# Graph attention on one core: another order for the products of the last pairs

## The chip, the cores and the metric

The kernel runs on one core of a Trainium2 chip. The metric is the device time of one execution in microseconds; the time before is the median of six runs. A core has TensorE (PE in the profile, its weight loads PEld), VectorE (DVE), ScalarE (ACT), GpSimd (POOL) and SyncE (SP), which here issues most DMAs and loads the registers that these DMAs take their addresses from.

## The reference

One layer of graph attention over 12,500 nodes with 256 features in 8 heads of 32, and 200,000 edges sorted by destination. The part that matters:

```python
h = maximum(layernorm(x), 0)
q, k, v = h @ Wq + bq, h @ Wk + bk, h @ Wv + bv        # 8 heads of 32
logits = sum(q[dst] * k[src], axis=-1) / sqrt(32)
expv = exp(logits - segment_max(logits, dst)[dst])
agg = segment_sum(expv / segment_sum(expv, dst)[dst] * v[src], dst)
out = agg + (h @ Wskip + bskip)
y = h + gelu(out)
result = x + layernorm(y) * gamma + beta
```

The last three lines, done for 128 nodes at a time, are what the change reorders at the end of the kernel.

## The kernel before, in words

First `project` makes h and the rows of k and v and stores them in the tables `h_tab` and `kv_tab`, while `make_plan` turns the edge list into indices. Then `walk_streams` goes over the edges. The edges are cut into 8 streams of 25,000, and each stream into chunks of 383 new edges, 66 chunks in all (`NST`, c from 0 to 65). A chunk is three tiles of 128 edges; the last one (c = 65) has only two (`KL`).

For each chunk GpSimd gathers rows of k and v (L1006), VectorE multiplies them with queries that TensorE has spread over the edges (L1039, L1049), sums them to logits (L1058), and takes running maxima of them (L1078 to L1081). TensorE transposes the logits before that (L1067) and the exponentials after it (L1089). VectorE multiplies v with the weights (L1105, L1110), and TensorE adds the weighted rows up per node (`add_up`, L1124), in three groups i = 0, 1, 2. ScalarE copies each group's sums to `sums_w` (L1133) and the last row on to the next chunk (L1139), and SyncE stores them to `table` in HBM (L1143). The addresses of these stores come from `nodes(c)`, a load of registers.

When the sums of 256 nodes are known to be complete, a `Pair` of two blocks of 128 nodes finishes them: sums, x and h are fetched (L797 to L799), and then

- `turn`: four transposes of h to PSUM (L812) and a copy to `hT` on ScalarE (L815)
- `divisors`, `divide`: VectorE divides the sums by the weights' sums (L804, L806, L818)
- `skip`: TensorE puts the bias (L825) and the product of hT with Wskip (eight matmuls, L829) into a PSUM bank
- `add`, `gelu`: four matmuls with the identity add the divided sums to that bank (L834), and ScalarE takes gelu (L838)
- `stats`, `root`, `factors`, `normal`: mean and variance on VectorE (L841 to L847), square root on ScalarE (L851), L855 and L856 on VectorE, the normalised rows on ScalarE (L861)
- `shifted`, `scale`, `store`: x + beta in PSUM (L868, L871), L875 and L877 on VectorE, and two stores to `out` by SyncE (L882)

There are 52 pairs, numbered 0 to 51. From chunk 10 on, a pair's fetch is put into a chunk, most of its work into the following one, and its end (`factors` to `store`) into the one after that. Pairs 0 to 45 are done in this way. In the loop's last iteration (c = 64) `before` is pair 43, `pair` is pair 44 and `pair_next` is pair 45. In the code after the loop, for chunk 65, `before` is pair 44 and `pair` is pair 45. Six pairs are left (46 to 51, called leftover 0 to 5 here), of the class `Last`, in the list `lasts`. Their sums are complete only when chunk 65 is stored. Their x and h are fetched during chunk 64 (`fetch_rows`, into buffers of the gathers that are no longer used), their sums after chunk 65's stores (`fetch_sums`, L909).

The order of all instructions but the gathers is written out by hand. `keep` ties every instruction to the one before it on the same engine, so each engine works strictly in the order of the code, and an instruction that waits holds up all that stands behind it on its engine. SyncE too takes its register loads (`loaded`, L770), its waits and its DMAs in the order of the code.

[...] A tile from `hot_ps` waits until the tile two allocations earlier has been read. The leftovers' products go to `qe_ps` (leftovers 0 to 3), `xt_ps` (4) and `ag_ps` (5); pair 45's product goes to `ag_ps`. Transposes of h, `shifted` and parts of `add_up` use `hot_ps`. The buffer `hT` of a pair has one copy (`bufs=1`), so a copy to it waits for the matmuls of the product before.

ScalarE has to load another table of functions when it goes from one function to another (1.28 us each, ACT_TABLE_LOAD in the timeline); `table_of` asks for such a load ahead of its use by a one-element instruction.

Of the kernel before, what the change touches and what calls it, by code (L numbers as in the profile page):

```python
# [38 lines left out]
P = 128  # L39
# [5 lines left out]
S = 8  # L45
# [695 lines left out]
def walk_streams(tc, N, HID, NST, KL, ident, idx, d0_row, slot_row, near, near_n, e_tab, pen_tab, h_tab,  # L741
# [32 lines left out]
    class Pair:  # L774


        own, depth = "", 2
# [30 lines left out]
        def turn(self):  # L808
            ps = self.ps_h()
            for b in range(2):  # L810
                for c in range(KC):
                    self.keep(nc.tensor.transpose(ps[:, b, c, :], self.h[:, b, c * P:(c + 1) * P],  # L812
                                                  ident))
            self.hT = self.pool.tile([P, 2, KC, P], F32, name="hT", bufs=1)
            self.keep(nc.scalar.copy(self.hT, ps))  # L815
# [63 lines left out]
        def store(self, b):  # L879
            if b == 0:  # L880
                self.nodes = loaded(slot_row[0:1, self.m, 0:2], N - P)
            self.keep(nc.sync.dma_start(out[ds(self.nodes[b], P), :], self.y[:, b, :]))  # L882

    class Last(Pair):

        own, depth = "_l", 4
# [14 lines left out]
        def fetch_rows(self):  # L901
            self.places()
            for b, node in enumerate(loaded(slot_row[0:1, self.m, 0:2], N - P)):
                self.keep(nc.sync.dma_start(self.x[:, b, :], x[ds(node, P), :]))
                self.keep(nc.sync.dma_start(self.h[:, b, :], h_tab[ds(node, P), :]))

        def fetch_sums(self):
            for b, row in enumerate(loaded(slot_row[0:1, self.m, 2:4], S * NT - P)):
                self.keep(nc.sync.dma_start(self.sums[:, b, :], tab[ds(row, P), :]))  # L909

    rest = []
    with ExitStack() as es:
# [199 lines left out]
        def add_up(c, i, tiles=range(K)):  # L1112
# [3 lines left out]
            if tiles[0] == 0:  # L1116
                g["ps", i] = (hot_ps.tile([P, 2 * HID], F32, name="ps_hot")
                              if i == 1 or i == 2 and c == NST - 1 else
                              ag_ps.tile([P, 2 * HID], F32, name="ps_a"))[:, :SUMS]
# [87 lines left out]
        for c in range(NST - 1):  # L1207
# [78 lines left out]
            add_up(c, 1)  # L1286
            if pair:
# [34 lines left out]
        if pair:  # L1322
            pair.turn()
            pair.divisors()
            pair.skip()
# [10 lines left out]
        for p in lasts[:2]:  # L1336
            p.turn()
            p.skip()
# [4 lines left out]
        weigh(c, tiles_of(c) - 1)  # L1343
        for i in range(3):
# [3 lines left out]
        for p in lasts:  # L1348
            p.fetch_sums()
        if pair:  # L1350
# [7 lines left out]
        for p in lasts[2:]:  # L1358
# [5 lines left out]
        for p in lasts:  # L1364
# [3 lines left out]
            p.gelu()  # L1368
        table_of(AF.Sqrt)
# [356 lines left out]
```

## Time and profile before

| | us |
|---|---|
| median of the six runs | 2408.04 |
| lowest and highest of them | 2404.53, 2420.95 |
| the profiled execution, its own time | 2412.02 |
| its span | 2410.2 |

Busy time by engine, from the page:

| engine | busy us | share of the span |
|---|---|---|
| TensorE matmul | 1885.8 | 78% |
| VectorE | 1934.9 | 80% |
| GpSimd | 1592.0 | 66% |
| ScalarE | 1078.6 | 45% |

TensorE's granted clock has two levels in this trace, 1.00 and 0.50; its mean over the span is 0.874. Eight matmuls of L829 took 1.99 us in a stretch at 1.00 and 3.78 us in one at 0.50.

The marks of the end, from the timeline, in us from the span's start:

| start | what |
|---|---|
| 2320.54 | L1124, group 1 of chunk 64 (1.56) |
| 2326.34 | L1124, group 2 of chunk 64 (2.91) |
| 2333.47 | L812, transposes of pair 45 |
| 2336.54 | L1082, chunk 65's exponentials (0.42) |
| 2339.67 | L1105, chunk 65's first tile |
| 2346.97 | L1124 of chunk 65, until 2350.29 |
| 2349.75 | L1143, first store of chunk 65's sums |
| 2359.22 | L909, first fetch of the leftovers' sums |
| 2370.14 | L834, add of leftover 0 |
| 2377.43 | L838, gelu of leftover 5 (0.60) |
| 2383.39 | L882, first store of the leftovers |
| 2405.41 | L882, last store |

In the timeline a line gives start, duration, engine, line, operation and tiles. SPq is SyncE's queue; PEld is a weight load, which overlaps the matmuls. The idle time before an instruction stands in brackets with what ended it.

### The profile page before, as it was taken

What the parts mean: (1) busy time and instruction counts of PE and PEld (TensorE: products, weight loads), DVE (VectorE), ACT (ScalarE), POOL (GpSimd) and SP (SyncE); (2) the same over time, 40 slices, a digit from 0 to 9 for tenths busy, and PEclk for the clock granted to TensorE, in tenths of its full rate; (3) what the DMA queues carried; (4) which work ended last, traced back from release to release, by engine and by line L of the source; (5) the groups of instructions that cost most, each with busy time, mean ns of one, the idle gap of its engine ahead of it and who ended that gap; (6) DMA issues with size and microseconds to landing.
All of it is one profiled execution on the core that took longest, in us unless ns stands there. A gap on an engine that the chain in (4) does not pass through costs nothing.

```text
span 2410.2 us, 34981 instructions
## 1 busy us (share of the span) xinstructions
PE 1885.8 (78%) x10240; PEld 1090.5 (45%) x10240; DVE 1934.9 (80%) x2228; ACT 1078.6 (45%) x2527; POOL 1592.0 (66%) x1646
## 2 busy tenths in 40 slices
PE   7999677778877777787787777877787778887775
PEld 3444444344544444444454444544444444444443
DVE  7888577778788888788778888788777888888864
ACT  3432233333455455454445454454454554544433
POOL 2210677777777777777777777777777777777720
PEclk9999768777899899899989898899888998889877
DMA  7865777778787887888878888788878888888852
GB/s 275 302 250 205 235 244 243 244 244 253 251 276 245 266 262 245 265 270 258 265 240 260 260 266 260 244 274 261 265 246 264 257 263 258 264 254 262 254 159 68
DMA packets 274030, 601.06 MB, mean 249 GB/s; under 512 B 47239, under 2 KB 164212, under 8 KB 271648
## 3 DMA queue, kind: packets, MB, share of 16 engines
q0 software_dynamic: 128736, 423.23, 56.2%
q1 hardware_dynamic: 144562, 175.02, 21.8%
q8 instruction: 84, 1.38, 0.2%
q14 instruction: 118, 0.97, 0.1%
q10 hardware_dynamic: 530, 0.47, 0.1%
HBM read 514.42 MB, written 84.11 MB: 248 GB/s over the span
## 4 chain that ended last, share of the span: by engine, by line
POOL 29%; DMA 21%; DVE 15%; issue 15%; PE 15%; ACT 4%; SPq 0%; DVEq 0%; ACTq 0%; POOLq 0%
POOL kv L1006 28%; DMA kv<-kv_tab,idx 17%; DVE vw L1105 5%; PE ps_kv L243 5%; DVE prod L1049 4%; PE ps_qe L1039 3%; DVE L L1058 2%; DMA table<-sums_w 1%; PE ps_a L829 1%; DMA x_in<-in_x_dram 1%; DVE st L845 1%; PE ps_hot L871 1%; PE ps_hot L999 1%; PE ps_a L1124 1%; DMA e_tab<-row 1%
## 5 line engine op out<-in xcount | busy, mean ns | idle before, releaser
L1006 POOL DMA_INDIRECT kv<-kv_tab,idx x1576 | 1548.7, 983 | 524.6 <-issue 431.6
L1039 PE MATMUL ps_qe<-qw,to_e 64*128 64x256 f32 x3152 | 475.4, 431 | 220.6 <-DVE prod L1049 220.5
L1105 DVE TENSOR_TENSOR vw<-ps_x,kv 128x2048 f32<-128x2048 f32 x197 | 444.6, 2284 | 173.7 <-ACT vw L1098 172.1
L1049 DVE TENSOR_TENSOR prod<-ps_qe,kv 128x1024 f32<-128x1024 f32 x394 | 467.5, 1219 | 120.5 <-DMA kv<-kv_tab,idx 104.3
L1039 PEld LDWEIGHTS ps_qe<-qw,to_e 64*128 64x128 f32 x3152 | 302.5, 203 | 374.8 <-DVE prod L1049 334.7
L1058 DVE TENSOR_REDUCE L<-prod 128x64 f32<-128x2048 f32 x197 | 450.4, 2286 | 6.7
L999 PE MATMUL ps_hot<-w_q,hwT 128*128 128x256 f32 x792 | 256.7, 470 | 1.0 <-ACT hwT L985 0.8
L1124 PE MATMUL ps_a<-vw,to_n 128*32 128x264 f32 (+1 forms) x2356 | 219.6, 399 | 2.7 <-DVE vw L1105 1.5
L999 PEld LDWEIGHTS ps_hot<-w_q,hwT 128*128 128x128 f32 x792 | 169.7, 230 | 90.7 <-issue 60.7
L243 PE MATMUL ps_kv<-w_kv,hT 128*128 128x512 f32 x392 | 186.8, 620 | 21.8 <-ACT hT L136 20.8
L1029 ACT ACTIVATE to_n<-ps_hot,ones 128x384 f32<-128x384 f32 x197 | 107.2, 579 | 212.7 <-PE ps_hot L1027 210.5
L1133 ACT COPY sums_w<-ps_a 128x264 f32<-128x264 f32 x131 | 49.7, 379 | 325.8 <-PE ps_a L1124 325.8
L946 ACT ACT_TABLE_LOAD x138 | 177.1, 1283 | 2.4
L1001 ACT COPY qw<-ps_hot 128x256 f32<-128x256 f32 (+1 forms) x132 | 63.3, 480 | 253.5 <-PE ps_hot L999 251.5
L1139 ACT COPY kv<-ps_a 1x264 f32<-1x264 f32 x390 | 144.1, 369 | 6.4
L1018 ACT ACTIVATE to_e<-ps_hot,ones 128x384 f32<-128x384 f32 x264 | 143.7, 587 | 6.8 <-PE ps_hot L1016 6.6
L1124 PEld LDWEIGHTS ps_a<-vw,to_n 128*32 128x32 f32 (+1 forms) x2356 | 88.5, 118 | 123.9 <-issue 75.7
L985 ACT COPY hwT<-ps_hot 128x256 f32<-128x256 f32 (+1 forms) x132 | 63.5, 481 | 166.7 <-PE ps_hot L982 162.8
L829 PE MATMUL ps_a<-w_s,hT 128*128 128x256 f32 x376 | 123.1, 483 | 12.9 <-ACT hT L815 10.4
L1016 PE MATMUL ps_hot<-et,near 48*128 48x384 bf16 x264 | 90.2, 342 | 42.2 <-ACT qw L1001 25.7
L243 PEld LDWEIGHTS ps_kv<-w_kv,hT 128*128 128x128 f32 x392 | 72.0, 194 | 105.8 <-issue 72.1
L1089 PE MATMUL ps_x<-ident,W 64*128 64x64 f32 x197 | 31.0, 275 | 98.1 <-ACT W L1082 98.1
(289 smaller groups left out, 2189.2 us busy)
## 6 DMA issues: line engine op xcount, KB each, us to landing
kv<-kv_tab,idx POOLq DMA_INDIRECT x1576
kv_tab<-kvo SPq DMA_DIRECT2D x14, 1536.0 KB
table<-sums_w SPq DMA_DIRECT2D x264, 65.0 KB
hw<-h_tab SPq DMA_DIRECT2D x264, 64.0 KB
pen<-pen_tab SPq DMA_DIRECT2D x66, 192.5 KB
sums<-table SPq DMA_DIRECT2D x92, 132.0 KB
x_f<-in_x_dram SPq DMA_DIRECT2D x92, 128.0 KB
h<-h_tab SPq DMA_DIRECT2D x92, 128.0 KB
```

What stands on the lines that cost most here:

```text
L243: ins = nc.tensor.matmul(ps_kv, hT[:, c, :], w_kv[:, c, :], start=c == 0, stop=c == KC - 1)
L829: self.keep(nc.tensor.matmul(self.ps[:, b, :], self.hT[:, b, c, :], w_s[:, c, :], start=False, stop=False, skip_group_check=True))
L946: keep(nc.scalar.activation(dummy[:, 1:2], dummy[:, 0:1], function))
L999: keep(nc.tensor.matmul(ps[:, b, :], g["hwT"][:, b, k, :], w_q[:, k, :], start=False, stop=k == KC - 1, skip_group_check=True))
L1006: nc.gpsimd.indirect_dma_start(out=t[:, s, :], out_offset=None, in_=kv_tab[:, :], in_offset=bass.IndirectOffsetOnAxis(ap=idx[:, s, j, c:c ...
L1018: keep(nc.scalar.activation(step[c]["to_e"][:, i, :], ps[:, :CH], AF.Relu, scale=-1.0, bias=ones))
L1039: keep(nc.tensor.matmul(ps[:, b, a, :], g["to_e"][r, 2 * half + a, j * P:(j + 1) * P], g["qw"][r, (half + a) * half, :], start=True, stop= ...
L1049: keep(nc.vector.tensor_tensor(g["prod"][:, four, :].rearrange("p (a b) d -> p a b d", a=2), g["qe", half].rearrange("p b a d -> p a b d") ...
L1058: keep(nc.vector.tensor_reduce(g["L"][:, j, :].rearrange("p (s h) -> p s h", s=S), g["prod"].rearrange("p s (h d) -> p s h d", h=HEADS), A ...
L1105: keep(nc.vector.tensor_tensor(t[:, :, HEADS:].rearrange("p s (h d) -> p s h d", h=HEADS), wj[:, :, :, None].to_broadcast([P, S, HEADS, D] ...
L1124: keep(nc.tensor.matmul(ps[at:at + w, :], g["to_n"][:, j, i * P + at:i * P + at + w], g["vw"][j][:, s, :], start=j == 0, stop=j == tiles_o ...
L1139: keep(nc.scalar.copy(step[c + 1]["kv"][0][0:1, s, HID - HEADS:], ps[at:at + 1, :]))
```

## The change

It concerns the end alone: chunk 64's second half and all that follows. No arithmetic is added or removed.

- Pair 45's transposes and its product with Wskip (`turn`, `skip`) move from the code after the loop into the loop's last iteration, behind group 1 of `add_up` for chunk 64. Group 2 of chunk 64 takes a tile of `hot_ps` and not of `ag_ps`.
- Leftover 0's transposes move ahead of chunk 65's maxima, its product stays behind pair 45's gelu; leftover 1's transposes follow that, and its product moves behind chunk 65's `add_up`, together with transposes and products of leftovers 2 and 3. Leftover 4 stays where leftovers 2 to 5 were, behind pair 45's end. Leftover 5's come after the gelu of leftover 1.
- The leftovers have four buffers for hT, of their own.
- The registers with the places of the leftovers' sums are loaded ahead of chunk 65's last `add_up` (`find_sums`), and the registers with the node numbers, loaded for the fetch of x and h, are kept for the stores.

```diff
     class Pair:
-        own, depth = "", 2
+        own, depth, turned = "", 2, 1
...
-            self.hT = self.pool.tile([P, 2, KC, P], F32, name="hT", bufs=1)
+            self.hT = self.pool.tile([P, 2, KC, P], F32, name="hT" + self.own, bufs=self.turned)
...
         def store(self, b):
-            if b == 0:
+            if b == 0 and not self.own:
                 self.nodes = loaded(slot_row[0:1, self.m, 0:2], N - P)
...
     class Last(Pair):
-        own, depth = "_l", 4
+        own, depth, turned = "_l", 4, 4
...
         def fetch_rows(self):
             self.places()
-            for b, node in enumerate(loaded(slot_row[0:1, self.m, 0:2], N - P)):
+            self.nodes = loaded(slot_row[0:1, self.m, 0:2], N - P)
+            for b, node in enumerate(self.nodes):
...
+        def find_sums(self):
+            self.rows = loaded(slot_row[0:1, self.m, 2:4], S * NT - P)
+
         def fetch_sums(self):
-            for b, row in enumerate(loaded(slot_row[0:1, self.m, 2:4], S * NT - P)):
+            for b, row in enumerate(self.rows):
...
-                              if i == 1 or i == 2 and c == NST - 1 else
+                              if i == 1 or i == 2 and c > NST - 3 else
...
             add_up(c, 1)
+            if c == NST - 2 and pair_next:
+                pair_next.turn()
+                pair_next.skip()
             if pair:
                 pair.stats()
...
         if pair:
-            pair.turn()
             pair.divisors()
-            pair.skip()
+        for p in lasts[:1]:
+            p.turn()
         maxima(c)
...
             pair.add()
             pair.gelu()
-        for p in lasts[:2]:
+        for p in lasts[:1]:
+            p.skip()
+        for p in lasts[1:2]:
             p.turn()
-            p.skip()
...
         weigh(c, tiles_of(c) - 1)
+        for p in lasts:
+            p.find_sums()
         for i in range(3):
             add_up(c, i, range(tiles_of(c) - 1, tiles_of(c)))
         if before:
             before.store(1)
         for p in lasts:
             p.fetch_sums()
+        for p in lasts[1:2]:
+            p.skip()
+        for p in lasts[2:4]:
+            p.turn()
+            p.skip()
...
             table_of(AF.Gelu)
-        for p in lasts[2:]:
+        for p in lasts[4:5]:
             p.turn()
             p.skip()
...
-        for p in lasts:
+        for i, p in enumerate(lasts):
             p.divisors()
             p.divide()
             p.add()
             p.gelu()
+            if i == 1:
+                for p in lasts[5:]:
+                    p.turn()
+                    p.skip()
```

## The prediction

> **What bounds the kernel now.** I read the page's chain of waits first, to see whether the change touches what sets the time of the loop.
>
> ```profile
> POOL kv L1006 28%; DMA kv<-kv_tab,idx 17%; DVE vw L1105 5%; PE ps_kv L243 5%; DVE prod L1049 4%; PE ps_qe L1039 3%; DVE L L1058 2%; DMA table<-sums_w 1%; PE ps_a L829 1%; DMA x_in<-in_x_dram 1%; DVE st L845 1%; PE ps_hot L871 1%; PE ps_hot L999 1%; PE ps_a L1124 1%; DMA e_tab<-row 1%
> ```
>
> The loop runs at the pace of the gathers (L1006 and their landing, 45% of the span). The change leaves them alone, and by the timeline the last gather is over by 2308. So only the end counts, from about 2320 to 2410.2, some 90 us of 2410.
>
> Second, SyncE's queue and its own waits from 2370 on (waited for: us in total, times, longest).
>
> ```profile
> 2383.39 22.35 SPq L882 DMA_DIRECT2D out_dram<-kv  x12
> SPq L882 <- DMA out_dram<-kv: 13.4, 11, 2.3
> SPq L882 <- DVE kv L877: 11.2, 1, 11.2
> ```
>
> The page's chain of waits stops at 2396.46, with the last L877, and so hides what really ends the span. The twelve stores of the leftover pairs go out one at a time: eleven waits, each for the store before to land. The first goes out at 2383.39, when the first leftover pair's L877 ends; the last at 2405.41; the span ends 4.8 us later. So the end is the first leftover store + 22.0 + 4.8, and the question is how much earlier the first L877 comes.
>
> Third, the chain of waits between 2350 and 2378 (start, us, what).
>
> ```profile
> 2353.89 1.28 ACT L946
> 2355.18 0.20 ACT dummy L946
> 2355.38 0.47 ACT hT L815
> 2355.90 2.79 PE ps_qe L829 x8
> ...
> 2359.63 0.59 ACT hT L815
> 2360.27 3.71 PE ps_qe L829 x8
> ...
> 2365.15 1.99 PE ps_x L829 x8
> ...
> 2368.31 1.99 PE ps_a L829 x8
> 2370.30 0.88 PE ps_qe L834 x4
> ...
> 2377.43 0.60 ACT kv L838
> ```
>
> What leads to that first store is TensorE with ScalarE: transposes, copy of hT, eight matmuls with Wskip, pair after pair. The sums are no part of it: the first L818 (divide) ends at 2363.21, while its add (L834) waits in TensorE's order until 2370.14.
>
> Fourth, TensorE's busy time and granted clock in stretches between clock changes (us; busy and count of PE, PEld, DVE, ACT, POOL; clock; DMA share; GB/s).
>
> ```profile
> 2322.82:2326.23 3.41, 0.11 (x1) 0.11 (x1) 3.34 (x4) 2.28 (x5) 0.00 (x0) 1.00 0.61 184
> 2326.23:2329.65 3.42, 3.42 (x15) 1.35 (x14) 0.01 (x1) 0.33 (x2) 0.00 (x0) 0.50 0.40 132
> 2329.65:2333.06 3.41, 1.29 (x6) 0.77 (x5) 0.69 (x1) 2.73 (x7) 0.00 (x0) 1.00 0.32 90
> 2333.06:2336.47 3.41, 3.27 (x10) 2.06 (x9) 2.65 (x7) 0.59 (x1) 0.00 (x0) 0.50 0.18 60
> 2356.95:2360.37 3.42, 3.23 (x11) 1.91 (x9) 0.00 (x0) 0.59 (x1) 0.00 (x0) 0.50 0.06 16
> 2360.37:2363.78 3.41, 3.41 (x8) 2.65 (x9) 1.29 (x4) 0.00 (x0) 0.00 (x0) 0.50 0.63 169
> ```
>
> After a stretch with little work the next runs at 0.50, and twelve L1124 matmuls take 2.91 us there against 1.56 just before. The hole at 2322 is where the change puts work.
>
> **The change, step by step.** All times are on the clock of this execution. It took 2412.0 us (span 2410.2, 1.8 outside); the median of the runs is 2408.04, 4.0 lower. I take the gain off both.
>
> (1) Pair 45's transposes and product move into the hole. TensorE is free at 2322.10; transposes 0.60, bias matmul 0.39 (full-clock rows). The copy of hT (0.59) queues on ScalarE behind L1139, which ends at 2323.45: done by 2324.05, product (1.99) until 2326.05; L1067 needs the engine at 2326.12. It costs nothing with 0.07 to spare; at half clock (3.78) it delays L1067 by 1.8. On ScalarE root and the table load slide by 0.6, under the idle 4.16 before L1133 at 2329.32. The PSUM bank of ag_ps is then held until pair 45's gelu, which is why L1124's last group for chunk 64 takes a bank of hot_ps; the two tiles before it there are already copied. The hole filled, those twelve matmuls should run at full clock: 2.91 becomes 1.56, **1.35 gained** (bounds: 1.35 gained, 1.8 lost). I take the gain, as 2.35 of 3.41 us is then busy, nearer to the stretches that keep the clock.
>
> (2) With that product gone from 2334 to 2339, the transposes back (L1089) no longer wait. Exp ended at 2336.96 and the first L1105 began at 2339.67. Now what follows Exp is ScalarE's own queue: table load 1.28, dummy 0.20, L1096 0.23, L1098 0.21, so L1105 starts 1.9 after Exp instead of 2.7: **0.8 gained**, 2.15 together. It starts at 2337.5.
>
> (3) TensorE then does pair 45's add (1.79 at half clock, row at 2307.80), leftover 0's product, leftover 1's transposes, and then L1124; leftover 1's product moves behind. Add from 2336.1 to 2337.9; product partly at half clock until 2341.1; transposes until 2341.8. L1124 starts there and not at 2346.97: 5.2 earlier, **3.05 more**. VectorE's weights are ready (second L1105 over by 2342.1; the second half of L1124 starts at 2343.4).
>
> (4) SyncE. Six loads of registers (0.47 each, up to 1.62) come before chunk 65's stores. Behind them stand chunk 65's node load and eight table stores; SyncE idled 14.1 us before the first. Six loads take 3 to 10 us from 2333.5, and the sums are ready at 2344.5: nothing, and even six long loads and the node load fit by 0.7. The fetches of the sums wait for the table stores to land, 9.5 after L1133 (2349.73 to 2359.22): they start at 2354.0. Without loads between them a pair takes 1.04, not 1.55: 2.6 gained on the sixth, but sums aren't late, so it is worth 0 here. Loads taken out between output stores (0.49, six) lie under the landing waits: 0 (bounds 0 and 0.6, since intervals with a load are 0.1 longer).
>
> (5) From the end of L1124 (2345.0 now, 2350.29 before) to the last gelu. Leftover 1's product 2.4; leftovers 2 and 3 at 3.16 each (period of the full-clock turns at 2340.34 and 2343.50); pair 45's x and beta (L868, L871) 1.5: 2355.2. Pair 45's root now stands behind hT of leftover 3 on ScalarE (2351.9): table load, root, factors, normal and Gelu table end at 2356.5, so leftover 4's hT is ready at 2357.1 and its product at 2359.1. Two adds with gelu between (1.03 + 0.65 + 1.03): 2361.8. Leftover 5: transposes, a copy behind the second gelu, product: 2365.1. Four adds with one gelu between: 2369.5; last gelu 2370.1. Before: 2378.03. This stretch shrinks from 27.7 to 25.1: **2.6 to 2.7**, by two half-clock stretches and a 3.4 us wait less, one product more. Four hT buffers instead of one cost space alone: the wait for the copy behind the product before is what they remove, and here TensorE's order hides it.
>
> The rest is as before: 5.36 from last gelu to first store, then 22.0 + 4.8. Sum: 1.35 + 0.8 + 3.05 + 2.7 = **7.9 us**. 2412.0 - 7.9 = 2404.1 for this execution, 2400 for the median.
>
> [...] The row: the stretch from 2329.65 had 1.29 us of work, and the next was still granted 0.50; so in (3) I count add and product at half clock, after a stretch of about the same fill. [...]
>
> **Rivals.** (B) *Full clock and an unhindered output queue.* Add and leftover 0's product at full clock give 0.76 + 0.2 + 1.2 = 2.2 more. Two of the eleven intervals between stores were 2.77 and 3.24 against 1.7 to 2.0; without these long landings 2.5 more. 7.9 + 4.7 = 12.6: 2395. For it: both are chance in this execution. Against: full clock needs the clock's free phase to fall well, and the long landings may return.
> (C) *The hole isn't filled.* If hT comes late on ScalarE or the product runs at half clock, L1067 goes 1.8 late and step (1) loses 3.2; half a stretch more lost elsewhere gives 3 to 5 gained: 2404. For: 0.07 us to spare. Against: the stretch began at clock 1.00.
> (D) *The slow end: TensorE's clock stays at half from 2341 to 2370.* Each product then costs 1.75 + 0.46 + 0.21 more, five are left (12.1), six adds 0.94 each (5.6), x and beta 1.1: 18.8 lost, 10.9 net, 2419. It makes the kernel slower from five half-clock stretches on (1.7 each) against 7.9. For: at 0.50 a stretch filled 3.23 of 3.42 did not recover. Against: from 2339.89 to 2356.95 five stretches in a row were full clock with the same mix of work, and the new order leaves fewer waits.
>
> **How the numbers follow.** Forecast (A) 0.44, from 2396 to 2403; B 0.34; C 0.13; D 0.09. What a measurement of this kernel can tell is about 0.5%, or 12 us: below 2396 and above 2420. Faster: 0.31 of B and 0.05 of A, 0.36. Slower: 0.06, the upper part of D with noise (the six runs shown lie from 2404.5 to 2421). Within: 0.58. The range, 2392.5 to 2408, holds A, most of B and C, and leaves out D and B's lower edge.
>
> **What would show it.** Right: pair 45's L829 between 2322 and 2327 by the loop's position, L1124's last group for chunk 64 at 1.6 us; the first L909 some 5 us earlier against the last L1058; the first leftover L882 7 to 9 us earlier; twelve stores still 1.7 to 1.9 apart. Wrong: L1067 waiting for L829 there; TensorE waiting for L909 sums ahead of the adds, which would make the fetch the bound; stores that no longer wait for one another, which would shorten the last 22 us and make 2400 too high.

## The result, and the profile after

The changed kernel took 2400.32 us (median of 22 runs, 2385.21 to 2407.36), the kernel before 2408.7 (48 runs, 2398.11 to 2420.95). The ratio is 0.9957 with a 95% interval of 0.9945 to 0.9969, some 10 us of 2409. The two profiled executions took 2412.02 and 2393.73 us, spans 2410.2 and 2391.9.

Those two spans lie 18.3 us apart, more than the medians. To see which part belongs to the change, all marks below are counted from M, the end of the last L1058 (the reduction for chunk 65's last tile): no moved instruction stands ahead of it on VectorE, and with it the loop is all but over. M is 2325.97 in the profile before and 2317.56 in the one after. So 8.4 of the 18.3 us are the loop, which varies from one execution to the next (M lay between 2315.96 and 2332.23 in four profiles of the changed loop: the one after, e7, e8 and e14), and 9.9 lie in the end. In the changed kernel lines stand a little lower: L1058 became L1062, L1067 L1071, L1089 L1093, L1105 L1109, L1124 L1128, L909 L913.

| us after M | before | after | gained up to here |
|---|---|---|---|
| L1124, group 2 of chunk 64, end | 3.28 | 1.84 | 1.4 |
| L1105, chunk 65's first tile, start | 13.70 | 11.06 | 2.6 |
| L1124 of chunk 65, start | 20.99 | 14.93 | 6.1 |
| L1124 of chunk 65, end | 24.32 | 18.26 | 6.1 |
| L909, first and last fetch of sums | 33.25, 41.60 | 27.22, 35.57 | 6.0 |
| last divide (L818), end | 45.00 | 38.91 | 6.1 |
| last gelu (L838), end | 52.06 | 42.70 | 9.4 |
| first store of a leftover (L882) | 57.42 | 48.06 | 9.4 |
| last store | 79.44 | 69.78 | 9.7 |
| end of the span | 84.26 | 74.33 | 9.9 |

First the timeline of the changed kernel, TensorE's part from the hole on (start, us, engine, line, operation, tiles; in brackets the idle time before and what ended it).

```profile
2315.65 1.99 PE L829 MATMUL ps_a<-w_s,hT 128*128 128x256 f32 x8 [1.10 <-ACT hT L815]
2317.61 0.30 PE L1071 MATMUL ps_x<-ident,L 128*64 128x128 f32 x1
2317.84 1.56 PE L1128 MATMUL ps_hot<-vw,to_n 128*64 128x264 f32 x12
...
2326.89 0.34 PE L1093 MATMUL ps_x<-ident,W 64*128 64x64 f32 x2 [2.89 <-ACT W L1086]
2327.15 1.31 PE L834 MATMUL ps_a<-o,ident 128*128 128x256 f32 x4
2328.40 0.60 PE L825 MATMUL ps_qe<-b_s,one_row 3*128 3x512 bf16 x1
2328.93 3.19 PE L829 MATMUL ps_qe<-w_s,hT_l 128*128 128x256 f32 x8
2331.96 0.60 PE L812 MATMUL ps_hot<-ident,kv 128*128 128x128 f32 x4
2332.49 0.66 PE L1128 MATMUL ps_a<-vw,to_n 128*32 128x264 f32 x8
```

Pair 45's product (first line) ends at 2317.64, 0.08 after M, and L1071 follows without a wait. The twelve matmuls of group 2 take 1.56 us instead of 2.91. Later the transposes back (L1093) wait for the exponentials, no longer for a product. Leftover 0's product is slow (3.19, where 1.99 is full speed), and chunk 65's sums follow at once.

Second, stretches of 3.41 us (in this trace and in the one before, changes of the granted clock lie whole multiples of 3.41 us apart; busy and count of PE, PEld, DVE, ACT, POOL; granted clock; DMA share; GB/s), still the changed kernel.

```profile
2314.32:2317.74 3.42, 2.32 (x10) 1.55 (x9) 3.35 (x4) 2.91 (x7) 0.00 (x0) 1.00 0.57 176
2317.74:2321.15 3.41, 2.24 (x15) 1.05 (x15) 0.08 (x1) 1.68 (x5) 0.00 (x0) 1.00 0.42 137
...
2324.57:2327.98 3.41, 1.09 (x6) 0.88 (x6) 2.34 (x5) 1.59 (x3) 0.00 (x0) 1.00 0.20 65
2327.98:2331.39 3.41, 3.41 (x9) 2.11 (x8) 2.77 (x3) 1.11 (x5) 0.00 (x0) 0.50 0.00 2
2331.39:2334.81 3.42, 3.42 (x34) 1.72 (x34) 3.38 (x6) 0.59 (x1) 0.00 (x0) 1.00 0.02 5
```

The stretch with the hole had 0.11 us of work before and has 2.32 now, and the next one keeps 1.00. From M until 0.1 us before the first leftover store one stretch runs at 0.50, after one with 1.09 us of work; in the kernel before, five did.

Third, SyncE's waits (in all, times, longest) in the end of the changed kernel.

```profile
SPq L882 <- DMA out_dram<-kv: 15.6, 11, 2.5
SPq L882 <- DVE kv L877: 7.8, 1, 7.8
```

As before: eleven waits of one store for the landing of the one before. The first store comes earlier, the chain behind it is as long as it was: 21.72 instead of 22.02.

### The profile page after: what moved, and what is told of

It reads as the page before. It is cut to its first block, busy times and chain, and to the rows that moved or that the text cites. A ratio compares the mean times of both kernels' runs of the same rounds, so it can differ in the third digit from the quotient of the medians.

```text
span 2391.9 us, 34967 instructions
## 1 busy us (share of the span) xinstructions
PE 1874.2 (78%) x10240; PEld 1083.1 (45%) x10240; DVE 1934.2 (81%) x2228; ACT 1077.7 (45%) x2527; POOL 1587.2 (66%) x1646
## 4 chain that ended last, share of the span: by engine, by line
POOL 31%; DMA 22%; issue 16%; DVE 14%; PE 13%; ACT 3%; SPq 1%; DVEq 0%; ACTq 0%; POOLq 0%
POOL kv L1010 30%; DMA kv<-kv_tab,idx 19%; PE ps_kv L243 5%; DVE vw L1109 5%; DVE prod L1053 4%; PE ps_qe L1043 2%; PE ps_a L829 1%; DVE L L1062 1%; PE ps_hot L871 1%; DVE st L845 1%; DMA x_in<-in_x_dram 1%; DMA e_tab<-row 1%; DVE sums L841 1%; DMA table<-sums_w 1%; ACT hT L136 1%
## 5 line engine op out<-in xcount | busy, mean ns | idle before, releaser
L1043 PE MATMUL ps_qe<-qw,to_e 64*128 64x256 f32 x3152 | 483.6, 437 | 218.9 <-DVE prod L1053 218.9
L1109 DVE TENSOR_TENSOR vw<-ps_x,kv 128x2048 f32<-128x2048 f32 x197 | 444.6, 2284 | 159.5 <-ACT vw L1102 159.5
L1043 PEld LDWEIGHTS ps_qe<-qw,to_e 64*128 64x128 f32 x3152 | 308.7, 206 | 375.7 <-DVE prod L1053 329.0
L1062 DVE TENSOR_REDUCE L<-prod 128x64 f32<-128x2048 f32 x197 | 450.4, 2286 | 6.8
L1128 PE MATMUL ps_a<-vw,to_n 128*32 128x264 f32 (+1 forms) x2344 | 219.7, 403 | 2.7 <-DVE vw L1109 1.5
L1128 PEld LDWEIGHTS ps_a<-vw,to_n 128*32 128x32 f32 (+1 forms) x2344 | 87.9, 119 | 125.7 <-issue 75.8
L829 PE MATMUL ps_a<-w_s,hT 128*128 128x256 f32 x368 | 108.8, 446 | 14.5 <-ACT hT L815 13.1
L1093 PE MATMUL ps_x<-ident,W 64*128 64x64 f32 x197 | 30.3, 271 | 101.1 <-ACT W L1086 101.1
```

Of the source, the lines that this page charges most:

```text
L829: self.keep(nc.tensor.matmul(self.ps[:, b, :], self.hT[:, b, c, :], w_s[:, c, :], start=False, stop=False, skip_group_check=True))
L1043: keep(nc.tensor.matmul(ps[:, b, a, :], g["to_e"][r, 2 * half + a, j * P:(j + 1) * P], g["qw"][r, (half + a) * half, :], start=True, stop= ...
L1062: keep(nc.vector.tensor_reduce(g["L"][:, j, :].rearrange("p (s h) -> p s h", s=S), g["prod"].rearrange("p s (h d) -> p s h d", h=HEADS), A ...
L1109: keep(nc.vector.tensor_tensor(t[:, :, HEADS:].rearrange("p s (h d) -> p s h d", h=HEADS), wj[:, :, :, None].to_broadcast([P, S, HEADS, D] ...
L1128: keep(nc.tensor.matmul(ps[at:at + w, :], g["to_n"][:, j, i * P + at:i * P + at + w], g["vw"][j][:, s, :], start=j == 0, stop=j == tiles_o ...
```

## The experiments

Two theories for the 9.4 us up to the first store stood against each other. By *order*, the new sequence shortens the path, at any clock. By *clock*, most of the gain is TensorE's clock: the change fills holes, or was lucky, and so has fewer half-speed stretches. Each part of the change was also tried alone, and the end chain was tested by itself.

In the first eight runs, e1 to e4 on one chip and e10, e11, e5 and e9 on another, the loop took some 1350 us longer, in the kernel before and in the variants alike (M between 3673 and 3706); why, stays open. Ratios there can hardly show 3 to 8 us. The end after M has no gathers and runs as in the first two profiles (group 2 takes 1.56 us, stores stand 1.7 to 1.9 apart but for the seventh and eighth interval), so verdicts rest on marks after M, of one profile each.

One thing differs in that end: where the clock's stretches fall. In the two profiles above, and in e7, e8 and e14, the granted clock was 1.00 from 6.4 to 6.7 us ahead of M on; in the other nine only from 4.8 to 5.0 ahead of it. Call these the early and the late position.

The runs, by first store after M and by time at 0.50 between M and that store:

| kernel | first store | at 0.50 | ratio to the kernel before on the same chip |
|---|---|---|---|
| before | 57.42 | 17.1 | 1 |
| after | 48.06 | 3.5 | 0.9957 [0.9945, 0.9969] |
| e1_early_only | 57.73 | 21.6 | 1.0014 [1.0000, 1.0028] |
| e2_late_product | 51.49 | 6.8 | 0.9990 [0.9973, 1.0007] |
| e3_buffers_registers | 54.52 | 11.5 | 1.0009 [0.9992, 1.0027] |
| e4_filled_hole | 55.17 | 10.2 | 1.0015 [0.9996, 1.0035] |
| e10_after_filled | 48.42 | 0 | 0.9994 [0.9974, 1.0015] |
| e11_before_filled | 53.84 | 0.7 | 0.9986 [0.9968, 1.0004] |
| e5_after_free_stores | 49.70 | 6.9 | 0.9978 [0.9963, 0.9994] |
| e9_two_rounds | 43.69 | 6.8 | 1.0001 [0.9983, 1.0020] |
| e13_early_filled | 53.86 | 0.7 | 0.9991 [0.9969, 1.0014] |
| e8_pinned_loads | 48.10 | 3.4 | 0.9980 [0.9962, 0.9999] |
| e14_slow_last | 48.06 | 3.4 | 0.9973 [0.9947, 0.9999] |
| e7_one_ht | 48.16 | 3.7 | 0.9991 [0.9969, 1.0014] |

### e1: pair 45's product early, nothing else

```diff
+            if c == NST - 2 and pair_next:
+                pair_next.turn()
+                pair_next.skip()
...
         if pair:
-            pair.turn()
             pair.divisors()
-            pair.skip()
```

(and group 2 of chunk 64 takes `hot_ps`, as in the change)

> The kernel before, with pair 45's transposes and product moved into chunk 64's hole as in the change, and nothing else. Marks are counted from the end of the last L1058 in each profile: before, the first leftover store went out at +57.4 and the span ended at +84.2; after, at +48.1 and +74.3. My theory (the hole takes the product for nothing, the clock of the matmuls behind it rises, and the transposes back come earlier): first L1105 of chunk 65 at +11.1 as after (before +13.7), first leftover store at +53.5 to +54.5, so 3 to 4 us of the 9.3. Rival, the order of the leftovers alone makes the gain: +57.4. Rival, the early product is the whole gain: +48. Ratio 0.998 to 0.999.

Measured: 57.73, no gain at all. The stretches of e1:

```profile
3682.15:3685.56 3.41, 1.26 (x7) 0.28 (x3) 0.69 (x1) 2.90 (x7) 0.00 (x0) 1.00 0.15 38
3685.56:3688.97 3.41, 2.10 (x5) 1.17 (x4) 1.24 (x4) 0.15 (x1) 0.00 (x0) 0.50 0.26 77
3688.97:3692.39 3.42, 1.40 (x4) 1.12 (x5) 2.04 (x4) 1.84 (x4) 0.00 (x0) 0.50 0.15 48
3692.39:3695.80 3.41, 3.27 (x10) 2.04 (x9) 3.08 (x3) 1.48 (x5) 0.00 (x0) 0.50 0.00 0
3695.80:3699.21 3.41, 3.41 (x11) 2.65 (x10) 3.11 (x6) 0.00 (x0) 0.00 (x0) 0.50 0.00 0
```

TensorE has little to do behind group 2 (1.26 of 3.41 us), and the clock falls. That alone isn't the move's doing: e3, below, with the old order on the same chip, has 1.08 us in the same place and falls too.

```profile
3700.32:3703.73 3.41, 1.08 (x5) 0.53 (x4) 0.69 (x1) 3.02 (x7) 0.00 (x0) 1.00 0.15 37
3703.73:3707.14 3.41, 3.27 (x11) 1.96 (x10) 2.10 (x5) 0.59 (x1) 0.00 (x0) 0.50 0.35 107
3707.14:3710.55 3.41, 3.41 (x10) 2.22 (x8) 1.18 (x3) 2.04 (x4) 0.00 (x0) 0.50 0.05 17
3710.55:3713.97 3.42, 3.01 (x15) 2.27 (x15) 3.04 (x3) 1.29 (x3) 0.00 (x0) 1.00 0.00 0
```

There the late product fills the next two stretches, and the clock is back. In e1 TensorE has nothing from 3687.7 to 3691.0, where the product was; the two stretches have 2.10 and 1.40 us of work, and the next one with 3.27 doesn't bring the clock back either: 13.7 us in a row at 0.50 instead of 6.8. So e1's first store is even 3.2 later than e3's (54.52).

### e2: the new order without the early product

```diff
(against the changed kernel)
-            if c == NST - 2 and pair_next:
-                pair_next.turn()
-                pair_next.skip()
...
         if pair:
+            pair.turn()
             pair.divisors()
+            pair.skip()
         for p in lasts[:1]:
             p.turn()
```

(group 2 of chunk 64 takes `ag_ps` again)

> The changed kernel, with pair 45's transposes and product put back to where they were before, and the last group of chunk 64 back on its old bank. If the two parts add up: first L1105 at about +13.7 as before, first leftover store at +51 to +52.5 (5 to 6 of the 9.3 us stay). Rival, the leftovers' order is worth nothing without the early product, because TensorE has no room: +55 or later. Rival, clock alone: the stretch from L1124 of chunk 65 to the last gelu is 27.7 as before where it was 24.5 after. Ratio 0.997 to 0.998.

Measured: 51.49, as expected, but not by the path expected. Chunk 65's first L1105 came later than in any other run, at 15.30. Its timeline (all engines):

```profile
3691.40 3.78 PE L829 MATMUL ps_a<-w_s,hT 128*128 128x256 f32 x8
...
3692.28 0.42 DVE L1085 TENSOR_TENSOR W<-ps_x,M 64x256 f32<-64x256 f32 x1
...
3694.97 0.71 PE L812 MATMUL ps_hot<-ident,kv 128*128 128x128 f32 x4
3695.71 0.58 ACT L815 COPY hT_l<-ps_hot 128x512 f32<-128x512 f32 x1 [4.37 <-PE ps_hot L812]
3696.20 0.41 ACT L1086 ACTIVATE W<-W 64x256 f32<-64x256 f32 x1
```

The maxima are ready at 3692.70, and the exponentials (L1086) start 3.5 us later: on ScalarE leftover 0's copy of hT stands ahead of them, it waits for leftover 0's transposes, and these stand behind pair 45's product on TensorE. So the two parts of the change belong together: leftover 0's transposes can stand ahead of the maxima without harm only because the product isn't there any more. The parts alone give -0.3 (e1) and 5.9 (e2), together 9.4, but these figures hold the clock's luck of each execution. Three runs with the stretches in the late position compare better: e3 with the old order (54.52), e2 (51.49), and e5 with the changed order (49.70; its free stores stand behind this mark). By them the new order is worth 3.0 without the early product and 1.8 more with it, the clock still included (11.5, 6.8 and 6.9 us at 0.50).

### e3: buffers and kept registers alone; e4: work without use in the hole

e3 gives the old order four hT buffers and keeps the node registers:

```diff
-            self.hT = self.pool.tile([P, 2, KC, P], F32, name="hT", bufs=1)
+            self.hT = self.pool.tile([P, 2, KC, P], F32, name="hT" + self.own, bufs=self.turned)
```

(and the change's edits for `turned` and `self.nodes`)

> The kernel before, with four hT buffers for the leftovers and the node registers kept from the fetch of x and h to the stores; order of the engines as before. My theory: nothing, first leftover store at +57.4 give or take 1, eleven intervals between the stores 21.5 to 22.0 in total (0 to 0.6 gained), end at +83.5 to +84.5. Rival, the buffers or registers make the gain: first store at +52 or earlier, or intervals under 1.6 each. Ratio 0.999 to 1.001.

e4 puts eight matmuls, whose result nobody reads, into the old order's hole:

```diff
             add_up(c, 1)
+            if c == NST - 2:
+                filler = hot_ps.tile([P, 2, HID], F32, name="ps_hot")
+                for k in range(8):
+                    keep(nc.tensor.matmul(filler[:, 0, :], ident, w_s[:, k % KC, :], start=True,
+                                          stop=True))
```

> The kernel before, with eight extra matmuls of the identity with Wskip in chunk 64's hole, whose product nobody reads; pair 45's product stays late. It tells the clock from the work: if step (1) is the clock, the twelve L1124 matmuls behind the hole take 1.6 to 2.0 us instead of 2.9 and the first L1105 comes at +12.2 to +12.6 (before +13.7, after +11.1); first leftover store 1 to 2 us earlier, +55.5 to +56.5. Rival, those matmuls were slow for another reason (bank, weight loads): 2.9 us again and no gain. Ratio 0.999 to 1.000.

Measured: 54.52 and 55.17. Both are 2 to 3 us under the profile before, with 11.5 and 10.2 us at 0.50 instead of 17.1, and in the same places (5.4 to 12.3 and 29.3 to 32.7 after M, for both; e3 has 1.3 more just ahead of the store). With the hole unfilled, e3's group 2 still took 1.56 us: in the late position the hole of the old order cost nothing. So e4 tells nothing of the filling as such; what it shows is that the old order's time depends on where the stretches fall. The expectation for e3 (57.4, give or take 1) missed by this. The buffers show no gain of their own.

### e10 and e11: both orders without a half-speed stretch

Matmuls without use keep TensorE busy in all holes. They write into a bank that the bias matmul then overwrites.

```diff
+        def fill(self, n):
+            if self.ps is None:
+                self.ps = self.ps_o()
+            for k in range(n):
+                self.keep(nc.tensor.matmul(self.ps[:, 0, :], ident, w_s[:, k % KC, :], start=True,
+                                           stop=True, skip_group_check=True))
```

The changed kernel gets four ahead of pair 44's `shifted` and seven behind leftover 0's transposes (e10); the kernel before gets ten in chunk 64's hole, six ahead of `shifted` and ten ahead of leftover 2's product (e11).

> The changed kernel with 11 extra matmuls of the identity with Wskip, written into leftover 0's bank and overwritten by its bias: four ahead of pair 44's x and beta (L868), seven behind leftover 0's transposes, both in gaps of TensorE of 1.3 and 2.9 us. They add work that nobody needs. If the granted clock carries a good part of the gain: no half-clock stretch between the last L1058 (the mark) and the last gelu, first leftover store at +46 to +47 (after +48.1, with one such stretch). If only the order counts: +48 to +49, or later by the extra work. Ratio, where the loop runs as before, 0.995 to 0.996.

> The kernel before, order unchanged, with 26 such extra matmuls: ten in chunk 64's hole into leftover 0's bank, six ahead of L868 into pair 45's, ten behind leftover 2's transposes into leftover 2's. By the half-clock stretches of the first profile (3.4, 6.8 and 6.8 us long), full clock takes 1.35 from L1124, 2.9 from pair 45's work and 3.2 from leftovers 2 and 3: 7.4. Theory now, after the early product alone gained nothing in a run with half clock from +5.4 to +19.1: the clock makes more than half of the gain, first leftover store at +49.5 to +52. Rival, the order makes it: +55 or later. The part of the order at full clock is the distance to the filled changed kernel, 3 to 5 us by the theory, 8 to 10 by the rival. Ratio 0.997 to 0.998.

Measured: 48.42 and 53.84; e11 lies between its theory (49.5 to 52) and its rival (55 or later). From M on, the stretch up to the first store in e10, and the one up to 0.7 us before it in e11:

```profile
3676.98:3725.40 48.42, 40.23 (x201) 27.35 (x200) 25.36 (x63) 22.59 (x45) 0.00 (x0) 1.00 0.26 72
```

```profile
3673.32:3726.46 53.14, 45.66 (x227) 31.66 (x226) 24.40 (x62) 22.28 (x44) 0.00 (x0) 1.00 0.23 66
```

The single stretches of e10, where the changed kernel alone has its slow one:

```profile
3682.37:3685.78 3.41, 3.41 (x18) 2.54 (x18) 1.54 (x4) 0.78 (x2) 0.00 (x0) 1.00 0.28 82
3685.78:3689.20 3.42, 3.42 (x17) 2.26 (x15) 1.74 (x4) 2.15 (x6) 0.00 (x0) 1.00 0.14 48
3689.20:3692.60 3.40, 3.24 (x23) 2.32 (x24) 3.38 (x3) 1.07 (x2) 0.00 (x0) 1.00 0.00 0
```

With the clock at 1.00 in both, the new order is 53.84 - 48.42 = 5.4 us ahead. The old order gains 3.6 us by filling (57.42 to 53.84); the new one gains nothing (48.06 to 48.42): its one slow stretch costs no more than the filler and a later L1067 (0.65 after M instead of 0.06, see step 1 below).

But the filler isn't free, and it costs the old order more. In e11 the exponentials end 11.63 after M, in e3, with the stretches in the same place and no filler, 9.90: x and beta (L868), behind the filler, start at 6.91 instead of 4.67. And leftover 2's product starts 0.9 after its hT is ready, since ten fillers are still running. That is 2.6 in all. In e10 L868 starts at 5.74, in e1 at 5.17: 0.6. An estimate without the filler's cost is thus 51.2 and 47.8, or 3.4 for order. So order alone is worth 3.4 to 5.4 of the 9.4 us, and the clock 4 to 6: the profile before had 17.1 us at 0.50, the one after 3.5. Neither theory stands alone.

### e13: the early product alone, with the clock kept up

e1 with four matmuls of filler ahead of `shifted`, eleven behind it, and ten ahead of leftover 2's product.

> The kernel before with pair 45's early product alone, and 25 extra matmuls (four ahead of L868, eleven behind L871, ten behind leftover 2's transposes) so that TensorE's gaps, also the one that the early product leaves behind, are filled. Theory: the early product gained nothing by itself because it left that gap and the clock fell from +5.4 to +19.1; at full clock it is worth about 1 us against the filled kernel before (first leftover store at +53.8, with L1067 1.4 late): +52.3 to +53.2. Rival, it is worth nothing at any clock: +53.8 or later. Rival, it is most of the order's 5.4 us: +50 or earlier.

Measured: 53.86, the same as e11 (53.84), with M at 2324.31, the loop as fast as in the first profiles. The exponentials end 1.2 earlier than in e11 (10.43 and 11.63), and yet chunk 65's L1124 starts at 19.48, in e11 at 19.47. In e13 the filler ended at 11.9 and so held the transposes back; pair 45's gelu and leftover 0's copy of hT then come when they do in e11 (gelu ends at 13.87 in both). Without that filler the gelu, which on ScalarE stands behind the exponentials, a table load (1.28) and three short instructions, could have ended at 12.7 at best (in e11 it ends 2.24 after the exponentials). So the early product is worth at most 1.2 us in the old order at full clock, and probably less, as e11's exponentials are late by its filler; no gain of it is shown.

### e8: the loads of the sums' registers really ahead

In the changed kernel's trace the loads of `find_sums` do not stand where the diff puts them. Each pair's load still comes between two pairs of fetches (2345.75, 2347.31 and so on), as in the kernel before: a load is put off until its registers are first used. e8 ties them to their place.

```diff
         def find_sums(self):
-            self.rows = loaded(slot_row[0:1, self.m, 2:4], S * NT - P)
+            loads, self.rows = nc.values_load_multi_w_load_instructions(
...
+                skip_runtime_bounds_check_because=IN_RANGE, bass_reorder=False)
+            for load in loads:
+                self.keep(load)
```

> The changed kernel with the six loads of the sums' registers pinned ahead of chunk 65's node load (in the changed kernel they stand between the fetches as before). By step (4): six loads in a row before chunk 65's first table store, that store not later, twelve fetches in 6 to 6.5 us from first to last in place of 8.35, the last divide 2 to 2.6 us earlier after the first fetch; first leftover store unchanged against its last gelu, gelus 0 to 0.6 earlier, ratio 0.995 to 0.999 where that can be seen. Rival, the sums' fetch is the bound: last gelu 2 us earlier after the first fetch (15.5 in the changed kernel).

SyncE's timeline, the twelve fetches: the kernel before, the changed kernel, and e8.

```profile
2359.22 8.68 SPq L909 DMA_DIRECT2D kv<-table  x12
```

```profile
2344.77 8.69 SPq L913 DMA_DIRECT2D kv<-table  x12
...
2365.62 22.05 SPq L882 DMA_DIRECT2D out_dram<-kv  x12
```

```profile
2343.14 6.08 SPq L917 DMA_DIRECT2D kv<-table  x12
...
2364.05 22.00 SPq L882 DMA_DIRECT2D out_dram<-kv  x12
```

Pinned, the twelve fetches take 6.08 us instead of 8.69, and the last divide ends 1.7 earlier after M (37.18 and 38.91; 2 to 2.6 were expected). The last gelu ends where it did, 42.73 and 42.70, and so does all behind it. The loads are worth nothing here: TensorE's order, with the products of leftovers 4 and 5 in it, sets the last gelu, and not the sums.

### e7: one buffer for hT

```diff
-        own, depth, turned = "_l", 4, 4
+        own, depth, turned = "_l", 4, 1
```

> The changed kernel with one buffer for the leftovers' hT in place of four. By step (5), space alone: no copy waits for a product that is not over already in TensorE's order, from the last sums copy (L1137) to the last gelu 24 to 25 us as in the changed kernel, first store within what the clock does (+47 to +50). Rival, the buffers let the copies go ahead: each of the five later products waits up to 2 us more, first store at +53 or later.

Measured: 48.16 against 48.06 for the first store, and every mark of the first table up to the last divide is the same within 0.02. The four buffers are worth 0.1 us: with one, leftovers 2 and 3 start their products 3.16 us after the one before, as in the kernel before, and with four after 3.11. The ratio, 0.9991 [0.9969, 1.0014], can't tell: the loop varies by more (M is 2327.85 in this profile, ten us later than in the profile after).

### e14: VectorE's end made late

Four extra multiplications into a tile that nobody reads any more stand ahead of the last two leftovers' `scale`.

```diff
             if i > 1:
+                if i > 5:
+                    for _ in range(4):
+                        keep(nc.vector.tensor_mul(lasts[i - 2].h, lasts[i - 2].g,
+                                                  gam[:, None, :].to_broadcast([P, 2, HID])))
                 lasts[i - 2].scale()
```

> The changed kernel with four extra multiplications of VectorE (0.69 us each, into a buffer no longer needed) ahead of the last L875 of each of leftovers 4 and 5. If the stores' chain is the end: the last L877 comes 5.5 us later (first store + 18.6 in place of 13.1), still ahead of its store, and the end stays at first store + 26.3 to 27. Rival, VectorE's last L877 sets the end: first store + 31.8.

VectorE's last work in e14:

```profile
2390.19 2.86 DVE L1400 TENSOR_TENSOR kv<-kv,gam 128x512 f32<-128x512 f32 x4
...
2393.87 0.69 DVE L877 TENSOR_TENSOR kv<-kv,ps_hot 128x512 f32<-128x512 f32 x1
2394.48 2.87 DVE L1400 TENSOR_TENSOR kv<-kv,gam 128x512 f32<-128x512 f32 x4
...
2398.17 0.69 DVE L877 TENSOR_TENSOR kv<-kv,ps_hot 128x512 f32<-128x512 f32 x1
```

The last L877 ends 66.63 after M, 5.5 later than in the changed kernel (61.13). The last store goes out at 71.30 instead of 69.78, and the end comes 1.7 later (76.01, 74.33), 27.95 after the first store, where 26.3 to 27 were expected. That comes from the landings (2.73, 3.67 and 2.61 us between stores, where the changed kernel had 2.36, 3.07 and 1.72): even in e14 the last L877 ends 2.1 before the store that it feeds (68.69). SyncE's waits in e14 name VectorE's L877 once, for the first store, as in the changed kernel:

```profile
SPq L882 <- DMA out_dram<-kv: 17.1, 11, 3.1
SPq L882 <- DVE kv L877: 7.8, 1, 7.8
```

So VectorE's last work can slide by 5.5 us; the landings, one after another, set the end.

### e5: eight of the twelve stores don't wait for each other

The stores of the first four leftovers write different blocks and are declared independent. The last two leftovers write one block again, so these four stores keep their waits; to free all twelve wasn't tried.

```diff
-            self.keep(nc.sync.dma_start(out[ds(self.nodes[b], P), :], self.y[:, b, :]))
+            put = self.keep(nc.sync.dma_start(out[ds(self.nodes[b], P), :], self.y[:, b, :]))
+            if self.own and self.m < rest[4]:
+                tc.declare_no_dep(put.ins, group="out_rows", reason="rows of different blocks")
+                tc.add_to_no_dep_group("out_rows", put.ins)
```

> The changed kernel; the eight stores of leftovers 0 to 3 don't wait for one another (their blocks are different rows here; the last four write one block again and keep their waits). If the end is the chain of landings: the eight go out within 0.6 us behind each L877, the twelve take 17 to 18 us from first to last in place of 21.7, and the end comes 4 to 4.5 us earlier, at first store + 22. Rival, as the page's chain of waits has it, the end hangs on VectorE's last L877: no change.

SyncE's waits in e5:

```profile
SPq L882 <- DVE kv L877: 12.2, 3, 7.9
SPq L882 <- DMA out_dram<-kv: 7.5, 5, 2.3
```

The waits for landings fall from 15.6 us to 7.5, and the free stores go out within 0.6 of their L877. But from first to last store it still takes 20.04 us instead of 21.72, and the end is 24.64 after the first store instead of 26.27: 1.6 gained, where 4 to 4.5 were expected. L877s of the first leftovers come only every 3.25 us, and the two slow landings moved on to the next stores (3.24 and 2.82). Freed of its landings, the chain is bound by VectorE up to the fourth leftover, which is 10.3 of the 20 us. The ratio, 0.9978 [0.9963, 0.9994], is the best on that chip, but the freedom holds only for an input whose leftover blocks lie as here. It is no better kernel in general.

### e9: the first two leftovers stored before the others' sums are added

```diff
+        table_of(AF.Sqrt)
+        end_of(lasts[:2], {1: lasts[2:4], 2: lasts[4:5], 3: lasts[5:]})
+        table_of(AF.Gelu)
+        for p in lasts[2:]:
+            p.add()
+            p.gelu()
         table_of(AF.Sqrt)
...
+        end_of(lasts[2:])
```

(`end_of` runs statistics to stores for some leftovers, with divides of the others in between)

> The changed kernel, all waits kept, with leftovers 0 and 1 finished and stored (root to stores) ahead of the adds and gelus of leftovers 2 to 5: two more table loads (2.9 us on ScalarE), the same work otherwise. If the end is the first store plus 22: first leftover store at +40 to +42 in place of +48.1, leftover 2's at +50 to +52, last store at +62 to +65 (after +69.8), end 5 to 7 us earlier than after, ratio near 0.993. Rival, the end is a matter of the engines' work: the extra table loads make it 2 to 3 us later than after.

Measured: the first store at 43.69, 4.4 earlier than in the changed kernel, and the end at 76.67, 2.3 later. ScalarE's timeline of e9:

```profile
3749.22 1.28 ACT L950 ACT_TABLE_LOAD   x1
...
3755.83 0.60 ACT L838 ACTIVATE kv<-ps_a 128x512 f32<-128x512 f32 x1 [1.09 <-PE ps_a L834]
3756.44 1.28 ACT L950 ACT_TABLE_LOAD   x1
...
3757.85 0.47 ACT L851 ACTIVATE rstd_l<-mv_l,eps 128x2 f32<-128x2 f32 x2
```

Two more table loads and four gelus stand between the two rounds. Leftover 2's first store goes out at 55.99, where in the changed kernel it did at 55.19; the chain has a gap of 5 us, and what was gained ahead of it is gone. These 0.8 us are a third of the 2.3; the rest is the seventh and eighth interval, 3.48 and 3.79 us here and 2.36 and 3.07 in the changed kernel. The rival's number came out, 2 to 3 us later, but only in part by the table loads. "The end is the first store and 26 more" holds only while no link of the chain waits for anything but a landing.

## Why the prediction was right

Forecast 2400, measured 2400.32, and the mechanism is the one of forecast A. That the two agree to 0.3 us is luck in part: the steps were too small by 2 in this pair of profiles, and one of them hangs on where the clock's stretches fall. By its own steps, all in us after M, so that the loop's varying time is out:

(1) *The hole.* Predicted 1.35, measured 1.44. The 0.07 us to spare became -0.08, and L1071 started 0.05 after M where L1067 had 0.15. The prediction didn't have a condition that the runs show. In the late position (e2, e3) group 2 takes 1.56 with the hole open and ends at 1.90 and 1.91; with the product in it (e1, e5, e9, e10, e13) the product ends 0.8 after M, L1067 starts at 0.62 to 0.68, and group 2 ends at 2.38 to 2.43. There the step loses 0.5 instead of gaining 1.4: a small form of rival C, which the 0.07 to spare had left open. That the first two profiles had the early position is luck.

(2) *L1105.* Predicted 2.15 with step 1, measured 2.64. What follows the exponentials is ScalarE's own queue, as worked out: 1.8 from the end of the exponentials to L1109.

(3) *L1124 of chunk 65.* Predicted 5.2 earlier, measured 6.1. Half of the difference is step 2; the rest is the add of pair 45, taken at half speed throughout (1.79), of which only the end fell into the slow stretch (1.31). Leftover 0's product took 3.19: the half-speed stretch that the step counted on was there, behind a stretch with 1.09 us of work.

(4) *SyncE.* The value, 0, is right; the mechanism failed. The sixth fetch was to come 2.6 earlier by shorter steps between fetches. They kept their 1.55 us a pair, since the loads didn't move: that step of the mechanism was wrong. e8 made the step true and showed that it is worth 0 even then. The six loads ahead of the stores did go; the intervals that had held one didn't shrink (1.81, 1.80, 1.87, 1.82 against 1.81, 1.81, 1.86, 1.83, leaving out the slow eighth), as bounded.

(5) *From L1124 to the last gelu.* Predicted 2.6 to 2.7, measured 3.3 (27.74 to 24.44). The terms were a little too long: a leftover's transposes and product took 3.11, not 3.16 (that is what the four buffers bring, by e7), x and beta 1.4, not 1.5, and leftover 4's product ended 13.6 after L1124, not 14.1. From the last gelu to the first store 5.36, in both. One reading was off without consequence: the last gather starts at 2308.32 and ends at 2309.27, still ahead of the end that the sum counts.

The sum of 7.9 was 2.0 too small against 9.9 in this pair of profiles. The comparison of medians gives 8.4, and the ratio 10.4 (7.5 to 13.2). The predicted time itself came out because 4.0 us were taken off for the median, which then stood at 2408.7 in more runs. On the chip of the last four runs three variants of the changed kernel (e8, e14, e7, ending 0.02, 1.7 and 1.0 us later after M) had ratios of 0.9980, 0.9973 and 0.9991, each with an interval of some 0.002 either way: 2 to 6 us. The changed kernel itself didn't run there. Whether the gain is smaller on that chip, or the kernel before had a luckier clock there, stays open; that e13, with the old order of the leftovers, had the late position there would fit the second.

The rivals. *B* wanted full clock for add and product, which didn't come, and a chain without long landings. Where the clock's stretches fall does vary between executions, as the argument against B had it (6.4 to 6.7 or 4.8 to 5.0 us ahead of M). The half with the landings was wrong in kind: the long landings are not chance. They are the seventh and eighth interval in every profile with one unbroken chain (after: 2.36, 3.07; e10: 2.63, 3.56; e13: 2.36, 3.97). B's other 2.2 us couldn't be had by filling either: e10, at full clock, had its first store at 48.42 instead of 48.06. *C* fell with the 1.56 us of group 2. *D* fell too: from 2331.39 to 2365.52 all stretches were granted 1.00. But e1 shows that its mechanism is real: four slow stretches in a row, in which the 1.1 us that L1105 had gained (12.60 instead of 13.70) were lost again.

What the prediction didn't separate is how much of the gain would be the clock's: it had clock in steps 1 and 5, and the runs make it 4 to 6 of 9.4.

## What to carry to other kernels

A part of a reordering can be worth nothing alone and something with the rest: a step moved away frees a place in the queue that another step must take, or else it leaves a hole and, as in e1, a slower clock (13.7 us in a row at 0.50). Compare marks relative to a common event near the change, and compare orders at a clock that filler holds constant, less what the filler itself costs, before calling a gain a gain of order. An earlier line in the source is not an earlier instruction: look in the trace whether the load has moved.

## What the runs showed of the hardware

**Slow stores beside instruction packets.** One 128 KB store takes 0.83 us from issue to its first packet, 0.5 for the packets, and 0.5 more until the next is issued (changed kernel, sixth store: 56.93, 57.76, 58.29, 58.80 after M). The slow seventh and eighth are slow in the packets. DMA queues in the changed kernel (packets, MB, share of 16 engines), first around the sixth store, then around the eighth:

```profile
q1 hardware_dynamic: 144, 0.13, 20.2%
```

```profile
q1 hardware_dynamic: 144, 0.13, 15.5%
q8 instruction: 1, 0.02, 1.9%
q14 instruction: 2, 0.02, 1.6%
```

Packets of 16384 and 8192 B on the instruction queues lie among the store's own. The first comes 1.5 us before TensorE's last matmul ends, in the profile before (68.25 and 69.76 after M), in the one after (58.93 and 60.40) and in e13 (64.66 and 66.20). So they go with the place in the program, not with the time, and follow the chain wherever it moves; in e5 the slow landings fall on other stores at that place. In the 13 profiles with twelve stores that wait for one another (156 stores), the packets of 28 took 0.7 to 2.5 us, and instruction packets overlapped each of them by 0.09 us or more; the packets of the other 128 took 0.51 to 0.53, with an overlap of 0.07 at most. In e14, whose program is a little longer there, one such packet falls on the eleventh store as well, whose packets take 1.28:

```profile
q1 hardware_dynamic: 144, 0.13, 15.1%
q14 instruction: 1, 0.01, 1.6%
```

Against 1.75 for an ordinary interval the two cost 1.9 us in the profile after and 2.5 in the one before. That the packets cause the delay rests on this coincidence, and wasn't isolated.

**The clock falls well before a stretch is idle.** Over the trace before from its first record of the clock (15.4 us) on, in stretches of 3.41 us, counted by TensorE's busy share: at 1.00, all 408 with at least 0.7 were followed by 1.00, 12 of 30 with 0.5 to 0.6, none of 23 under 0.4. At 0.50, of 61 with 0.9 or more, but not all, busy 15 were followed by 1.00, of 45 filled wholly 42, of 29 with 0.7 to 0.9 only one. So in this trace some 0.7 of a stretch kept the clock, while only a nearly full one brought it back, and a stretch of e1 with 3.27 us of work did not.
